# A delta-net kernel's slot order, written anew so that TensorE changes its tile shape four times instead of seven

## The chip, the core and the metric

The kernel runs as one program on one core of a Trainium2 chip. The core has engines that run side by side, each through its own queue in program order: TensorE (PE, matmuls and transposes into PSUM), VectorE (DVE), ScalarE (ACT), GpSimd (POOL) and SyncE (SP, which issues the DMA transfers here). The metric is the time of one execution on the device in microseconds (us). The kernel before takes 4227.17 us, the median of three runs between 4226.82 and 4233.79.

## The reference

The input `x` is 4 sequences of 1024 tokens with 256 channels. It goes through an attention layer of the gated delta-net kind and a feed-forward layer, each between layer norms and with a residual:

```
x = x + layernorm(attn(layernorm(x)))
x = x + layernorm(ffn(layernorm(x)))
```

The attention projects 256 channels to q and k (16 heads of 128 each) and v (32 heads of 128), runs a convolution of four taps over time and a silu, and normalizes q and k. A sequence is cut into 16 chunks of 64 tokens. For each head and chunk, with a lower triangular matrix `A` made of k, beta and a decay, it needs the inverse `Tm` of (1 - A), and then walks through the chunks with a 128 x 128 state:

```
v_new = u_i - kcd_i @ St
out_i = (q_i * exp(g_i)) @ St + attn @ v_new
St    = St * exp(g_last) + (k_i * exp(g_last - g_i)).T @ v_new
```

where `u` is `Tm @ (v * beta)` and `kcd` is `Tm @ (k * beta * exp(g))`. The output is normalized over its 128 channels, multiplied with silu(z), and projected back to 256 channels. The feed-forward layer has 688 inner channels, with weights that are looked up in a table of 16 values. All is float32.

## The kernel before, in words

**Tiling.** Work goes by groups of four v heads (eight groups). A *step* is one chunk of two sequences for one group: 32 steps in a group, 256 in all. The two pairs of sequences alternate, so a step's state was written two steps earlier. Eight steps are a *super block* (32 of them). Two chunks of 64 rows, of two sequences, share the 128 partitions. So many of the matmuls use only a part of TensorE's 128 x 128 array, and several run in it side by side: the profile writes the part as the *tile shape*, rows * columns, such as 64*64.

**Work as generators.** Each piece of work is a Python generator that emits instructions up to its next `yield`. The loop from line 1179 on makes one *slot* per step, and resumes the generators in the order of a string from `SLOTS` (lines 1014 to 1023; eight strings, one for each place in a super block, chosen by `iq`). Each name that goes through `go` counts as a place; a stage that yields a number is resumed by itself so many places later (`resume`, `go`, lines 970 to 990). Under the manual schedule each compute engine gets its instructions in the order in which they are emitted.

**The names in the strings.** A and B are `channel` (line 406): A makes a block of v, B of q or k, many slots ahead. Each has eight matmuls `pp` (128*128), ScalarE's `cv`, and three VectorE instructions of the convolution (line 456) that are resumed later (`far`, then 1). The step (line 780) has the stages N0 (transposes `pv`, and `x0`), N1 (`pkqs`, k and q against the state, then `x0` and `qs`), N2 (`px`, the inverse times x0, then `xs`; here also the transposes of k and ScalarE's `kt`), O3 (`po` and `core`), J (squares of `core`, for the norm), O4 (`pu`, and two places later the new state). N0 to N2 belong to this slot's step, O3, J and O4 to the step before. Z, T and U are `project_out` (line 919) of an older step: `pz` and `zs`, transposes `pto`, and `pout`. Lower-case names: s is `scores` (with `kkq`), n `norms`, v the inverse's rank-one updates on VectorE (`invert`), c `join` and b `build`, which put the inverse together from its blocks in five stages each, with DMAs through memory between them; r and q are the norm's roots on POOL.

**PSUM.** One pool has four banks, which `bank()` hands out in a ring (line 93): each new tile takes the bank of the one four before it, and waits until that has been read. Another has two double banks, for `pp` and `pu` (line 96).

**Loads.** `expand` (line 769) issues the three loads that a step needs, `ue`, `ae` and `qku`, for the next step: at a slot's start, or behind O4 for the first step of a super block.

Of the kernel before, what the change touches and what calls it, by code (L numbers as in the profile page):

```python
# [65 lines left out]
def delta_net_ffn_kernel(  # L66
# [258 lines left out]
    with ExitStack() as main:  # L325
# [80 lines left out]
        def channel(k, blk, n, far):  # L406
# [48 lines left out]
            for i in reversed(range(H)):  # L455
                V.scalar_tensor_tensor(cv, ps[:, :, i : i + BT], cw[:, ch, i : i + 1], cv, ALU.mult, ALU.add)  # L456
                if i == H - 1:
                    yield 1
# [309 lines left out]

        def expand(k, u):

            ue = sc.tile([P, HG, C], F32, tag="ue", name="ue", bufs=NZ)
# [4 lines left out]
            qku = sc.tile([P, 2, 2, MG, C], F32, tag="qku", name="qku", bufs=2)  # L776
            nc.sync.dma_start(qku.rearrange("p j a m t -> p j (a m t)"), k.qkd[:, :, u].rearrange("p j a m t -> p j (a m t)"))
            k.qku[u] = qku

        def step(k, u):  # L780
# [13 lines left out]
            x0 = t4("x0")  # L794
# [4 lines left out]
            if not first:  # L799
# [14 lines left out]
                qs = t4("qs")  # L814
# [5 lines left out]

            ue, ae = k.exp.pop(u)

            pxs = [bank("px") for _ in range(2)]
            if not last:
                for ab in range(2):
                    T_.transpose(pxs[ab][:, 2 * P : 3 * P], qk[:, 0, ab].rearrange("p m t -> p (m t)"), ident)  # L826
# [13 lines left out]
            if not last:  # L840
                kt = sc.tile([P, 2, 2, P], F32, tag="kt", name="kt")
                for ab in range(2):
                    for n in range(2):
                        A.activation(
                            kt[:, ab, n, :],
                            pxs[ab][:, 2 * P : 3 * P],
                            AF.Copy,
                            scale=k.cd[:, ab, blk, un, n : n + 1],
                        )
            yield  # L850
            pos = [bank("po") for _ in range(MG)]
            for n in range(2):
                for m in range(MG):
                    for ab in range(2):
                        T_.matmul(  # L855
                            pos[m][ab * C : (ab + 1) * C, n * P : (n + 1) * P],
                            lhsT=ae[m * C : (m + 1) * C, ab, n, :],
                            rhs=xs[m * C : (m + 1) * C, ab, n, :],
                            start=True,
                            stop=True,  # L860
                        )
            core = t4("core", OUT_LAG)
            for m in range(MG):
                two = slice(2 * m, 2 * m + 2)
                po = pos[m][:, : 2 * P].rearrange("p (h d) -> p h d", h=2)
                if first:
                    V.tensor_copy(core[:, two], po)
                else:
                    V.tensor_tensor(core[:, two], po, qs[:, two], ALU.add)  # L869
            k.cores[u] = core  # L870
            yield
            junk = sc.tile([P, P], F32, tag="junk", name="junk")
            for h in range(HG):
                A.activation(junk, core[:, h, :], AF.Square, accum_out=k.ms[:, u, h : h + 1])  # L874
            yield
            if not last:
# [17 lines left out]
                else:  # L894
                    flat = S_.rearrange("p m a h d -> p (m a h) d")
                    made = pu.rearrange("p a (n d) -> p (a n) d", d=P)
                    for i in range(2 * HG):
                        V.scalar_tensor_tensor(  # L898
                            flat[:, i, :], flat[:, i, :], el[:, ti, i : i + 1], made[:, i, :], ALU.mult, ALU.add
                        )  # L900

# [94 lines left out]
        older, gated, started = None, None, {}  # L996

        def work(kind, n, *args):
# [16 lines left out]
            "c A O3 s N0 n J O4 N1 Z T B n N2 U n s c",  # L1015
            "A O3 N0 J O4 N1 r Z s T B N2 q U c",
            "c A O3 N0 J O4 N1 b Z s T B N2 n U b",
            "A O3 N0 J v1 O4 N1 Z T B N2 U s b",
# [159 lines left out]
        with tc.manual_schedule(engines=COMPUTE):  # L1178
            for s in range(-LQ, len(units)):
# [5 lines left out]
                for c in "01234":  # L1185
                    gens["N" + c], gens["O" + c] = newer, older
# [128 lines left out]
```

## Time and profile before

| | before |
|---|---|
| median of three runs | 4227.17 us |
| the profiled execution, its own time | 4219.99 us |
| its span, first to last instruction | 4218.3 us |
| granted TensorE clock, mean | 0.979 |
| first step's `pv`, last step's `pv` | 252.1 us, 3894.4 us |
| TensorE busy | 3949.9 us |
| VectorE, ScalarE, POOL busy | 2972.5, 2810.3, 1964.5 us |

The profile shows one execution. Busy time is the time in which an engine had an instruction running. Matmuls overlap, and the ends that are shown for them are modelled; what TensorE can do is read better from the starts, one group to the next. A line of the timeline has the start and the length of a group of equal instructions in us, the engine, the line of the kernel, the operation, the tile written and those read, for TensorE its tile shape, and the number of instructions; in brackets, the idle time of the engine before it and what ended that. A line of the list of waits has who waited for whom, the total in us, how often, and the longest.

### The profile page before, as it was taken

To read this page: it belongs to the slowest core of one execution; us is meant where nothing else is said; L and a number is where in the kernel's file an instruction comes from. 1 tells how busy PE (TensorE), PEld (TensorE's weight loads), DVE (VectorE), ACT (ScalarE), POOL (GpSimd) and SP (SyncE) were. 2 spreads that over 40 slices of the span, in tenths; PEclk is the share of its full clock that TensorE was granted. 3 is DMA by queue.
4 is the path that set the end of the run, shared out by engine and by line. 5 is a ranking of instruction groups with operands and counts; after the bars stand their busy time and mean duration, and the time that the engine had idled before them with its cause. 6 is when DMAs were issued, how large, how long until landed. Compare 5 with 4: busy or idle time off the path is not lost.

```text
span 4218.3 us, 96596 instructions
## 1 busy us (share of the span) xinstructions
PE 3949.9 (94%) x34688; PEld 2683.1 (64%) x34688; DVE 2972.5 (70%) x7123; ACT 2810.3 (67%) x7509; POOL 1964.5 (47%) x1808
## 2 busy tenths in 40 slices
PE   3679999999999999999999999999999999999999
PEld 2356666666666666666666666666666666665454
DVE  4577787777777777777777877777777777676143
ACT  2467777777677777777777777777777767665211
POOL 2544555555455545555454555545454334334122
PEclk7889999999999999999999999999999999999999
DMA  3555556565555556665565556655656556553011
GB/s 103 147 126 128 125 134 139 135 143 139 132 145 138 134 133 142 152 138 132 137 148 139 129 139 148 143 134 139 142 141 143 131 132 144 137 130 97 25 46 25
DMA packets 1454779, 539.39 MB, mean 128 GB/s; under 512 B 1119440, under 2 KB 1414496, under 8 KB 1453920
## 3 DMA queue, kind: packets, MB, share of 16 engines
q1 hardware_dynamic: 1454304, 533.20, 53.4%
q8 instruction: 280, 4.59, 0.5%
q14 instruction: 195, 1.60, 0.1%
HBM read 292.82 MB, written 239.62 MB: 126 GB/s over the span
## 4 chain that ended last, share of the span: by engine, by line
PE 73%; DVE 7%; DMA 7%; SPq 4%; ACT 3%; issue 2%; POOL 2%; POOLq 0%; ACTq 0%; DVEq 0%
PE pp L439 17%; PE pout L950 11%; PE pkqs L806 8%; PE pz L145 8%; PE pu L882 5%; PE pgu L1115 4%; PE px L830 3%; PE po L855 3%; DVE cv L456 3%; PE pto L943 3%; DMA ndh<-nbh 3%; PE pv L793 3%; PE py L1131 2%; PE kkq L574 2%; PE px L826 1%
## 5 line engine op out<-in xcount | busy, mean ns | idle before, releaser
L456 DVE SCALAR_TENSOR_TENSOR cv<-pp,cw,cv 128x512 f32<-128x512 f32 x1536 | 1150.7, 749 | 563.4 <-ACT cv L453 527.8
L937 POOL TENSOR_TENSOR zs<-zs,rr 128x512 f32<-128x512 f32 x256 | 267.1, 1043 | 956.4 <-ACT zs L935 956.4
L439 PE MATMUL pp<-xnT,wq 128*128 128x262 f32 x2048 | 509.7, 391 | 49.5 <-DVE cv L456 30.3
L950 PE MATMUL pout<-wo,oT 128*128 128x256 f32 x2048 | 525.4, 401 | 30.0 <-POOL wo L387 14.1
L453 ACT ACTIVATE cv<-pp,cw 128x512 f32<-128x512 f32 x512 | 353.1, 690 | 290.1 <-PE pp L439 285.4
L439 PE MATMUL pp<-xnT,wv 128*128 128x262 f32 x2048 | 519.5, 396 | 26.5 <-DMA wv<-in_wqkv 24.8
L145 PE MATMUL pz<-wzs,xnT 128*64 128x512 f32 x2048 | 484.9, 594 | 6.7 <-DVE core L869 4.6
L898 DVE SCALAR_TENSOR_TENSOR S<-S,dkm,pu 128x128 f32<-128x128 f32 x1792 | 481.0, 342 | 0.0
L806 PE MATMUL pkqs<-S,qku 128*64 128x256 f32 x3840 | 467.7, 385 | 0.7 <-DVE core L869 0.4
L950 PEld LDWEIGHTS pout<-wo,oT 128*128 128x128 f32 x2048 | 378.2, 194 | 123.3 <-ACT cv L453 21.5
L439 PEld LDWEIGHTS pp<-xnT,wv 128*128 128x128 f32 x2048 | 383.8, 193 | 106.4 <-issue 37.7
L439 PEld LDWEIGHTS pp<-xnT,wq 128*128 128x128 f32 x2048 | 373.5, 192 | 111.5 <-issue 45.1
L869 DVE TENSOR_TENSOR core<-po,qs 128x256 f32<-128x256 f32 x480 | 181.2, 418 | 277.1 <-PE po L855 250.2
L874 ACT ACTIVATE junk<-core 128x128 f32<-128x128 f32 x1024 | 315.9, 309 | 54.9 <-DVE core L869 30.2
L806 PEld LDWEIGHTS pkqs<-S,qku 128*64 128x64 f32 x3840 | 254.1, 136 | 134.7 <-issue 1.2
L939 POOL TENSOR_TENSOR zs<-zs,core 128x512 f32<-128x512 f32 x256 | 326.7, 1276 | 20.0
L915 POOL TENSOR_TENSOR rr<-rr,rsqrt 128x16 f32<-128x16 f32 x64 | 187.1, 2923 | 280.3 <-DVE rr L907 280.0
L317 POOL TENSOR_SCALAR lt<-lx,lutb 128x344 f32<-128x344 int32 (+2 forms) x210 | 277.0, 1319 | 16.6
L797 ACT ACTIVATE x<-pv,nnk 128x256 f32<-128x256 f32 x512 | 214.7, 471 | 101.9 <-PE pv L793 100.7
L627 DVE TENSOR_TENSOR v<-v,rank 128x30 f32<-128x30 f32 (+7 forms) x480 | 268.8, 560 | 16.5
L882 PE MATMUL pu<-xs,kt 64*128 64x128 f32 x3840 | 278.9, 285 | 1.0 <-DVE cv L456 1.0
L558 POOL TENSOR_TENSOR dc<-dc,dkm 128x512 f32<-128x512 f32 x128 | 133.8, 1045 | 311.9 <-DMA dc<-rows_d 288.7
(191 smaller groups left out, 6820.5 us busy)
## 6 DMA issues: line engine op xcount, KB each, us to landing
qkd<-qk SPq DMA_DIRECT2D x256, 256.0 KB
qku<-qkd SPq DMA_DIRECT2D x256, 256.0 KB
dc<-rows_d SPq DMA_DIRECT2D x128, 256.0 KB
ltd<-lT SPq DMA_DIRECT2D x128, 256.0 KB
atd<-aT SPq DMA_DIRECT2D x256, 128.0 KB
ae<-atd SPq DMA_DIRECT2D x256, 128.0 KB
ue<-ued SPq DMA_DIRECT2D x256, 128.0 KB
acc_d<-ac SPq DMA_DIRECT2D x128, 256.0 KB
```

Of the source, the lines that this page charges most:

```text
L145: T_.matmul(ps[ab * C : (ab + 1) * C, :], lhsT=xnT[:, kc, 2 * p + ab, H + n * C : H + (n + 1) * C], rhs=rhs(kc), start=kc == 0, stop=kc == ...
L317: G_.tensor_scalar(o[:n, :cols], ix[:n, :cols], float(e), lutb[:n, e : e + 1], ALU.is_equal, ALU.mult)
L439: T_.matmul(ps[:, 2 * p : 2 * p + 2, : H + BT], lhsT=wt[:, kc, :], rhs=xnT[:, kc, 2 * p : 2 * p + 2, c0 : c0 + H + BT], start=kc == 0, sto ...
L453: A.activation(cv, ps[:, :, H : H + BT], AF.Copy, scale=cw[:, ch, H : H + 1])
L456: V.scalar_tensor_tensor(cv, ps[:, :, i : i + BT], cw[:, ch, i : i + 1], cv, ALU.mult, ALU.add)
L627: V.tensor_tensor(to, to, t, ALU.subtract)
L806: T_.matmul(as4(ps)[ab * C : (ab + 1) * C, two, :], lhsT=qk[:, j, ab, m, :], rhs=S_[:, m, ab], start=True, stop=True,)
L874: A.activation(junk, core[:, h, :], AF.Square, accum_out=k.ms[:, u, h : h + 1])
L882: T_.matmul(as4(pu[:, m])[:, 2 * ab + n, :], lhsT=kt[half, ab, n, :], rhs=xs[half, ab, n, :], start=True, stop=True,)
L898: V.scalar_tensor_tensor(flat[:, i, :], flat[:, i, :], el[:, ti, i : i + 1], made[:, i, :], ALU.mult, ALU.add)
L939: G_.tensor_tensor(zs, zs, k.cores.pop(u), ALU.mult)
L950: T_.matmul(pp[:, :HID], lhsT=oT[:, h, :], rhs=wo[:, h, :], start=h == 0, stop=h == HG - 1)
```

## The change

The order within a slot is written anew, and the step is cut into other stages: N0, N1, then X, Y and P for the step before, then O and K for the step before that.

- X is new: it takes the two banks `po`, transposes k into their columns 256 to 383, and makes `kt` from there (four ScalarE instructions). Before, these were part of N2 and used the `px` banks.
- Y is `px` and `xs`. P is `pu` and, two places later, the new state; it now stands before O in the step's order, and at the end of the slot.
- O is `po` and `core`, one slot later than before; it writes columns 0 to 255 of the banks that X of the next step has taken, which are handed over in the list `spare`. K is the squares.
- `x0` and `qs` get two buffers, `qku` three, `ue` two instead of three. `expand` is split: `fetch_qk` loads `qku` for the next step, and `expand` loads `ue` and `ae` for this slot's step, at its start or, for a super block's first step, at its end.
- U belongs to a step one older than T's.
- A's convolution is resumed three places after A instead of two.
- The stages of the inverse (v, c, b), of the scores and of the norms stand in other places, the last ones of `join` and `build` further from one another.

```diff
-        def channel(k, blk, n, far):
+        def channel(k, blk, n, far, near):
...
-                    yield 1
+                    yield near
...
+        def fetch_qk(k, u):
+            qku = sc.tile([P, 2, 2, MG, C], F32, tag="qku", name="qku", bufs=3)
+            nc.sync.dma_start(qku.rearrange("p j a m t -> p j (a m t)"), k.qkd[:, :, u].rearrange("p j a m t -> p j (a m t)"))
+            k.qku[u] = qku
+
         def expand(k, u):
-            ue = sc.tile([P, HG, C], F32, tag="ue", name="ue", bufs=NZ)
+            ue = sc.tile([P, HG, C], F32, tag="ue", name="ue", bufs=2)
...
-            x0 = t4("x0")
+            x0 = t4("x0", 2)
...
-                qs = t4("qs")
+                qs = t4("qs", 2)
...
             yield
 
+            banks = [bank("po") for _ in range(MG)]
+            spare[:] = [banks]
+            if not last:
+                kt = sc.tile([P, 2, 2, P], F32, tag="kt", name="kt")
+                for ab in range(2):
+                    T_.transpose(banks[ab][:, 2 * P : 3 * P], qk[:, 0, ab].rearrange("p m t -> p (m t)"), ident)
+                for ab in range(2):
+                    for n in range(2):
+                        A.activation(
+                            kt[:, ab, n, :],
+                            banks[ab][:, 2 * P : 3 * P],
+                            AF.Copy,
+                            scale=k.cd[:, ab, blk, un, n : n + 1],
+                        )
+            yield
             ue, ae = k.exp.pop(u)
             pxs = [bank("px") for _ in range(2)]
-            if not last:
-                for ab in range(2):
-                    T_.transpose(pxs[ab][:, 2 * P : 3 * P], qk[:, 0, ab].rearrange("p m t -> p (m t)"), ident)
...
+            yield
             if not last:
-                kt = sc.tile([P, 2, 2, P], F32, tag="kt", name="kt")
...
+                pu = two_banks("pu")
...
+                yield 2
+                state = S_.rearrange("p m a h d -> p (m a h d)")
...
             yield
-            pos = [bank("po") for _ in range(MG)]
+            pos = spare.pop() if spare else [bank("po") for _ in range(MG)]
...
         SLOTS = [
-            "c A O3 s N0 n J O4 N1 Z T B n N2 U n s c",
-            "A O3 N0 J O4 N1 r Z s T B N2 q U c",
-            "c A O3 N0 J O4 N1 b Z s T B N2 n U b",
-            "A O3 N0 J v1 O4 N1 Z T B N2 U s b",
-            "A b O3 s N0 n J O4 N1 Z v1 T B n N2 v1 U v1 n s",
-            "A v1 O3 N0 v1 J O4 N1 r Z s v1 T B N2 q v1 U b",
-            "A v1 O3 N0 v1 J O4 N1 Z s v1 T B N2 n v1 U",
-            "A v1 O3 N0 v1 J O4 N1 Z v1 T B N2 v1 c U s",
+            "v1 B N0 n s U c T A n X O Y N1 K Z s P c",
+            "B N0 U T A X O Y N1 K q Z s c P",
+            "B N0 U T A X O Y K N1 r Z s c n P",
+            "B N0 c U T A X O Y N1 K Z b n s P",
+            "v1 b B N0 n s U T A n X O Y N1 K Z s v1 b v1 P",
+            "B N0 v1 U b T v1 A X O Y N1 v1 K Z s v1 b P",
+            "B N0 U v1 T A v1 X O Y K N1 v1 r Z s v1 n P",
+            "B N0 U v1 T A v1 X O Y N1 v1 K Z v1 n s P",
         ]
...
-                    gens["A"] = channel(supers[nv], iv // 4, 2 * MG + iv % 4, 2)
+                    gens["A"] = channel(supers[nv], iv // 4, 2 * MG + iv % 4, 3, 1)
...
-                inv = work(invert, nq - 1)
+                inv = work(invert, nq - 1 if iq >= 4 else nq - 2)
...
-                if ahead and ahead[1]:
-                    expand(*ahead)
+                if 0 <= s + 1 < len(units):
+                    fetch_qk(*units[s + 1])
+                if s >= 0 and i:
+                    expand(*units[s])
...
-                older = newer
+                if s >= 0 and not i:
+                    expand(*units[s])
+                older, oldest = newer, older
...
-            drain(older)
+            for gen in (older, oldest, older, oldest):
+                go(gen)
+            drain(oldest, older)
```

## The prediction

> **What bounds the kernel now.** I read the page first (busy shares), then the idle time of each engine, then the list of waits, then TensorE's timeline of one slot in the middle, and last the starts of its single matmuls there.
>
> ```profile
> PE 3949.9 (94%) x34688; PEld 2683.1 (64%) x34688; DVE 2972.5 (70%) x7123; ACT 2810.3 (67%) x7509; POOL 1964.5 (47%) x1808
> ```
> TensorE is busy 94%; nothing else passes 70%. Between the first step's transposes (252 us) and the last step's (3894 us) TensorE idles little, and the slots repeat to within hundredths of a us. One whole slot, from one `pkqs` to the next, in TensorE's timeline (start, length, engine, line):
>
> ```profile
> 2014.30 1.95 PE L806 MATMUL pkqs<-S,qku 128*64 128x256 f32 x16
> 2016.08 1.89 PE L145 MATMUL pz<-wzs,xnT 128*64 128x512 f32 x8
> 2017.90 0.66 PE L943 MATMUL pto<-ident,zs 128*128 128x128 f32 x4
> 2018.39 1.93 PE L439 MATMUL pp<-xnT,wq 128*128 128x262 f32 x8
> 2020.16 0.38 PE L826 MATMUL px<-ident,qku 128*128 128x128 f32 x2
> 2020.47 0.67 PE L830 MATMUL px<-x,ue 64*64 64x128 f32 x16
> 2021.07 1.99 PE L950 MATMUL pout<-wo,oT 128*128 128x256 f32 x8
> 2022.90 1.93 PE L439 MATMUL pp<-xnT,wv 128*128 128x262 f32 x8
> 2024.76 0.67 PE L855 MATMUL po<-xs,ae 64*64 64x128 f32 x16
> 2025.36 0.66 PE L793 MATMUL pv<-ident,vt 128*128 128x128 f32 x4
> 2025.94 1.16 PE L882 MATMUL pu<-xs,kt 64*128 64x128 f32 x16
> 2027.04 1.95 PE L806 MATMUL pkqs<-S,qku 128*64 128x256 f32 x16
> ```
> Read the starts: each group begins where the one before stops feeding, so a slot is the sum of TensorE's groups, 12.74 us here. The column behind the tile names is the tile shape; it changes seven times. `pp` of `wq` has its own shape on both sides and takes 20.16-18.39 = 1.77; `pp` of `wv`, followed by 64*64, takes 1.86.
>
> The waits that remain are few:
>
> ```profile
> PE px L826 <- ACT zs L935: 39.8, 22, 4.5
> ...
> PE pp L439 <- DMA wv<-in_wqkv: 24.8, 7, 4.0
> ...
> PE px L826 <- DVE aT L585: 10.5, 7, 1.9
> ```
>
> **What a change of shape costs.** From the single starts in that window, against the spacing inside a group. Leaving: `wv` to `po` 311 ns for 221, so 90; a 64*64 group's last round 220 for 109, so 111; `pv` to `pu` 202 for 109, so 93; `pu` to `pkqs` 208 for 112, so 96; `pz` to `pto` 1.818 us for 1.717 where `kkq` (same shape) follows, so 101; `px` transposes to `px` 93. Entering (the first instruction is further from the second): 64*64 51, `pv` 56, `pu` 102, `pkqs` 51, `pto` 57, `pout` 104, and `pp` behind a 128*32 group 104. Old slot: leaving 90+111+93+96+101+93+111 = 695, entering 51+56+102+51+57+51+104 = 472, together 1.167 us. New slot "B N0 U T A X | O Y | N1 Z s | P": `pu` to `pp` 96+104, X to O 93+51, Y to N1 111+51, Z or s to P 101+102, together 0.709. **Saved 0.458 us x 256 steps = 117 us.** The 128*32 groups: `mh1`, `mh2`, `m1` stood inside 128*128 work and now stand between two shapes that change anyway (0.2 saved each), `m2` the other way round (0.2 lost); 2 x 0.2 x 32 super blocks = 13. TensorE alone: **-130 us**.
>
> **What is added on the path.** X of step n-1 transposes into columns 256 to 383 of the two banks that O of step n-2 then writes in columns 0 to 255, and O follows X directly in all eight slots. Between them in program order stand four ScalarE reads of those banks (`kt`). Before, `kt` read the `px` banks after TensorE had written all it would, so the trace shows no read by ScalarE ahead of a TensorE write into other columns of its bank. From below the price is nothing, if only touched columns count. From above, O waits for all four reads. The nearest row is in the gates, where L274 and L276 both only read one bank, ScalarE and VectorE:
>
> ```profile
> 80.13 0.60 ACT L274 ACTIVATE dk<-pgate 128x512 f32<-128x512 f32 x1 [19.23 <-PE pgate L272]
> ...
> 80.76 0.69 DVE L276 COPY dk<-pgate 128x512 f32<-128x512 f32 x1 [2.86 <-ACT dk L274]
> ...
> 86.07 0.69 DVE L276 COPY dk<-pgate 128x512 f32<-128x512 f32 x1 [4.62 <-ACT dk L274]
> ```
> VectorE needs nothing that ScalarE makes there, the matmul had landed at 80.09, VectorE was idle, and yet it starts 33 ns behind ScalarE's end, both times. Two engines hold one bank in turn even for reading, so I take the upper end. These rows touch the same columns; that is what they leave open. The Trainium skill ("PSUM — Partial Sum Buffer", section on bank collisions) says that two engines on one bank and partition quadrant collide also at disjoint columns and that software must keep them apart. By that rule the wait is certain; by rows of the same columns alone the sum could be the first rival's, 4090.
>
> The wait's length, with the rows of an old slot:
>
> ```profile
> 2007.63 0.69 ACT L453 ACTIVATE cv<-pp,cw 128x512 f32<-128x512 f32 x1 [0.64 <-PE pp L439]
> ...
> 2008.45 0.66 ACT L839 ACTIVATE xs<-px 128x256 f32<-128x256 f32 x2
> ...
> 2009.00 1.15 ACT L844 ACTIVATE kt<-px,cd 128x128 f32<-128x128 f32 x4
> ...
> 2012.80 0.76 DVE L869 TENSOR_TENSOR core<-po,qs 128x256 f32<-128x256 f32 x2 [0.16 <-PE po L855]
> ```
> Call the start of X's first transpose 0. A's `pp` ends at 0.16 and `cv` (ScalarE, emitted in A, so ahead of `kt`) runs 0.20 to 0.89. The four `kt` (1.15, overlapping their forerunner by 0.11 as behind `xs`) end at 1.91. TensorE restarted 53 ns after ScalarE's end wherever it waited for it, so O runs from 1.96. Then N1: its first bank is O's first (the ring of four banks goes po, po, px, px, pkqs), so it needs the first `core`. `core` starts 0.77 after `po` starts and its first half takes 0.42: 3.2 at most, 2.9 if O's first half, needing only two of the four `kt`, went ahead. TensorE's own path (O's rest, Y 0.55) gives 2.85. Without the wait N1 would start at 0.31+0.49+0.55 = 1.35. **Stall 1.55 to 1.85, I take 1.7** per slot. In slots 0 and 4 a norm's transposes (4 x 0.109) stand between A and X, so 1.26 there. Behind the waiting `po` on TensorE stand Y, N1, Z, the scores and P; what they feed (`xs`, `x0`, `qs`, `zs`, S) comes later by as much, and no other engine is the bound, so it adds nothing. Steps without `kt` (16 of 256, the end of each group) have none. 180 x 1.7 + 60 x 1.26 = 382: **+382 us**. VectorE's bound on this wait: `core` is emitted ahead of A's conv (due three places after A, behind O), and VectorE's earlier work in the slot (state update 2.15, B's conv 2.32, `ac` 0.41) fits into the 6.6 us from B to X, so it isn't late.
>
> **What the change gives back.** The 39.8 us row comes from `lb`'s copy (L708): ScalarE idled 75.7 us in 32 such copies for the load of `v` from `ndh`, with `zs` queued behind. Between that load and the copy stood A, O3, N0, O4, N1 = 5.8 us; now U, T, A, X, the stall, O, Y, N1, Z = 10.4 us, and 75.7/32 = 2.4 was missing. So that goes. With the waits of `px` and `pout` for `aT`, `oT`, `xs` (10.5+7.8+7.8) and about 1.5 us less in each of seven waits for `wv`, it is 75; I keep 40 to 120 (the other groups' idle may come or stay). Moved DMAs: `qku` is fetched in the same slot as before or earlier, and `ue`, `ae` one slot later for a use one slot later. For a super block's first unit `ue` has 8.7 us instead of about 19; the only wait for it so far is 2.4 us, once, so 0 (32 x 2.4 = 77 if that cover went). SyncE has idle time ahead of each. POOL gets no new work: `rms` and the table pieces (1.3+0.7) move within its slot, at 47%. The squares (1.61) now stand between `qs` and `zs` on ScalarE; `zs` is read by T a slot later, over 5 us of TensorE work behind Z. State update: emitted behind the next slot's B, and N1 that reads it is seven places on, 7 us for 2.15. One more stage in the pipe adds at the end a `po`, `core` and squares, 5 us.
>
> **Sum**, against the profiled execution's 4220.0 (span 4218.3; the median is 7 above): 4220-130+382-75+5 = 4402, and at the median **about 4405 us, 4% slower**.
>
> **Rivals.** (1) *Banks are only kept apart by columns touched*: O runs straight behind X. Left is N1's wait for the first `core`, 1.24 after O's start against 1.04 of O and Y, 0.2 x 256 = 50; 4220-130+50-60+5 = 4085, faster by 3%. For: no row shows different columns. Against: the gates' rows. It decides as soon as the stall per slot stays below some 0.8 us (130+75 over 256). (2) *The wait is there, but shorter, and everything else comes back*: 1.25 per slot (`kt` right behind the transposes, `cv` not ahead) is 180 x 1.25+60 x 0.81 = 274; with 120 back, 4249; within 0.2% only if nearly all 186 us of stalls of the old steps vanish. Against: `cv` is in program order ahead. (3) *VectorE gets in the way as well*: a conv part (0.75) or a rank-one pair of the inverse ahead of `core`, stall 2.1 or more: 180 x 2.1+60 x 1.66 = 478, 50 back, 4525. Against: 70% busy, now with longer slots.
>
> **How the numbers follow.** Forecast 0.80; rival 1 0.12; rival 2 0.04, of which 0.02 within 0.2%; rival 3 0.04. 0.2% (8 us) is about what a measurement of this kernel tells from no change. Faster 0.12, same 0.02, slower 0.86. The range goes from rival 2's 4250 to rival 3's 4520; what it leaves out is rival 1 and the far ends.
>
> **What would show it.** Right: in the new timeline `po` starts some 1.6 us after the `kt` transposes' end, with "ACT kt" as what ended TensorE's idle time, 300 to 450 us of it in the list of waits; slots of about 14 us; four shapes a slot; no `px` behind `zs`. Wrong: `po` 0.2 us behind the transposes while `kt` still runs; then the first rival. If `pkqs` waits for `core` by more than 0.5 us, the third.

## The result, and the profile after

The changed kernel takes 4764.45 us (median of 4 runs, 4754.37 to 4769.12), the kernel before 4226.99 us beside it: a ratio of 1.1264, with a 95% interval of 1.1243 to 1.1286. It is slower, as forecast, but by 537 us where the forecast had 178.

The busy line of the page after, with its span:

```profile
span 4752.7 us, 95765 instructions
...
PE 4109.1 (86%) x34688; PEld 2827.2 (59%) x34688; DVE 2915.6 (61%) x7123; ACT 2779.7 (58%) x7509; POOL 1961.2 (41%) x1808
```

The other engines are busy for as long as before or a little less; their shares fell because the span grew. TensorE is busy for 4109 us where it was 3950, with the same number of instructions and fewer changes of shape. So its instructions look longer, and it also idles more: 644 us instead of 268. Both have to be explained.

TensorE's list of waits, after (engine, what it was about to do, what ended the idle time: us in total, how often, the longest):

```profile
PE po L885 <- ACT kt L832: 289.7, 239, 4.9
PE m L735 <- DMA pad<-vtd: 70.1, 13, 10.3
PE m L735 <- ACT dc L562: 43.6, 10, 5.1
PE m L735 <- DMA pad<-ued: 35.1, 8, 4.9
```

The first row is the wait that the prediction priced. The next three are one wait, that of `m1` in `build`: 31 times, once per super block, 149 us. Before, `m1` waited only once, for 5.0 us. (`dc` is named where it came last by the profile; `m1` reads `mt` and `pad`, not `dc`.) The row `px` behind `zs` of before is down from 39.8 to 0.8 us, as forecast, and `pp` behind the load of `wv` is gone.

One slot of after in TensorE's timeline, an eighth string (start, length, engine, line, tiles, shape; in brackets the idle time before and what ended it):

```profile
2007.25 0.38 PE L829 MATMUL po<-ident,qku 128*128 128x128 f32 x2
2008.72 1.06 PE L885 MATMUL po<-xs,ae 64*64 64x128 f32 x14 [1.08 <-ACT kt L832]
...
2010.33 1.95 PE L809 MATMUL pkqs<-S,qku 128*64 128x256 f32 x16
2012.11 1.89 PE L145 MATMUL pz<-wzs,xnT 128*64 128x512 f32 x8
2013.92 1.16 PE L861 MATMUL pu<-xs,kt 64*128 64x128 f32 x16
2015.01 2.03 PE L439 MATMUL pp<-xnT,wq 128*128 128x262 f32 x8
2016.89 0.60 PE L796 MATMUL pv<-ident,vt 128*128 128x128 f32 x4
```

ScalarE's timeline at the same place:

```profile
2007.48 0.67 ACT L453 ACTIVATE cv<-pp,cw 128x512 f32<-128x512 f32 x1
2008.05 1.13 ACT L832 ACTIVATE kt<-po,cd 128x128 f32<-128x128 f32 x4
```

`po` starts 1.47 us behind X's first transpose, in the middle of the four `kt`: behind the two that read the first bank. Its first matmul waits for the semaphore that the second `kt` updates; its fifth, the first into the other bank, waits again, for the fourth. So it is the program that keeps `po` back, bank by bank; whether the chip would need it, no run shows. From X's first transpose to `pkqs` it is 3.08 us here.

The slots, as medians of the time from one `pv` to the next over 232 steps (the 4th to the 235th, called the middle steps from here on), by the string (us, worked out from the starts in the traces), and their sum:

| string | 1st | 2nd | 3rd | 4th | 5th | 6th | 7th | 8th | 232 steps |
|---|---|---|---|---|---|---|---|---|---|
| before | 15.10 | 14.82 | 15.09 | 14.95 | 14.32 | 14.12 | 13.61 | 12.73 | 3361.3 |
| after | 15.19 | 16.12 | 15.85 | 14.00 | 23.66 | 18.13 | 17.40 | 14.01 | 3836.8 |

The strings also hold other parts of the inverse and of the norms than before, so a comparison by place is rough and only the sum is strict. The first four are within 1.3 us of those of before; the fifth is 9.3 us longer, the sixth and seventh 4 us each. The stall per slot, which the prediction spread evenly, isn't what sets these three apart.

The fifth slot's `m1` in TensorE's timeline:

```profile
2096.16 1.94 PE L735 MATMUL m<-pad,mt 128*32 128x128 f32 x32 [4.19 <-DMA pad<-vtd]
2098.03 1.79 PE L861 MATMUL pu<-xs,kt 64*128 64x128 f32 x16
```

What SyncE issued ahead of it (its DMA queue, after; the second number is the time that the issues take):

```profile
2079.15 0.34 SPq L709 DMA_DIRECT2D vtd<-lb  x1
...
2085.84 5.97 SPq L614 DMA_DIRECT2D lb<-ltd  x4
2091.86 2.29 SPq L726 DMA_DIRECT2D pad<-vtd  x4
2094.19 2.62 SPq L730 DMA_DIRECT2D pad<-ued  x4
```

The same queue of before, a super block's build there:

```profile
2067.09 0.34 SPq L709 DMA_DIRECT2D vtd<-lb  x1
...
2074.98 2.24 SPq L726 DMA_DIRECT2D pad<-vtd  x4
2077.26 2.62 SPq L730 DMA_DIRECT2D pad<-ued  x4
...
2082.58 3.39 SPq L614 DMA_DIRECT2D lb<-ltd  x4
```

Before, the loads of `pad` were issued 7.9 us behind the store of `vtd`, ahead of the inverse's four `lb` loads. After, it is 12.7 us, behind them: the fifth string says "v1 b", and the `v1` issues the `lb` loads, 5.97 us of SyncE's time. `m1` then starts 4.3 us behind the first `pad` issue; before, the median was 8.3 us. TensorE stands still for 4.19 us, and everything in the slot behind it too.

Last, the granted clock. The view of stretches has, for each: its window, its length, the busy time and instructions of PE, PEld, DVE, ACT and POOL, the granted TensorE clock, and the DMA share and rate. After, around that `m1`:

```profile
2092.00:2096.00 4.00, 0.00 (x0) 0.00 (x0) 0.87 (x2) 3.88 (x12) 3.35 (x4) 0.99 0.96 139
2096.00:2099.40 3.40, 3.24 (x44) 2.89 (x46) 2.50 (x3) 1.08 (x2) 3.30 (x4) 0.50 0.77 143
```

Behind the empty 4 us TensorE gets half the clock for 3.4 us (0.50 in the last column but two). So `m1` takes 1.87 us from its start to that of `pu`, and `pu` runs 1.79 us instead of 1.16. That is one source of the longer busy time. The other is `po`, shown with 1.06 us instead of 0.67 because it waits inside for the second half of `kt`.

### The profile page after: what moved, and what is told of

The parts are those of the page before. It is cut to its first block, busy times and chain, and to the rows that moved or that the text cites. A ratio compares the mean times of both kernels' runs of the same rounds, so it can differ in the third digit from the quotient of the medians.

```text
span 4752.7 us, 95765 instructions
## 1 busy us (share of the span) xinstructions
PE 4109.1 (86%) x34688; PEld 2827.2 (59%) x34688; DVE 2915.6 (61%) x7123; ACT 2779.7 (58%) x7509; POOL 1961.2 (41%) x1808
## 4 chain that ended last, share of the span: by engine, by line
PE 53%; ACT 22%; SPq 7%; DVE 7%; POOL 4%; issue 4%; DMA 3%; ACTq 0%; DVEq 0%; POOLq 0%
PE pp L439 11%; PE pkqs L809 9%; PE pout L954 5%; PE pz L145 5%; ACT kt L832 5%; PE pgu L1119 4%; ACT cv L453 3%; PE pu L861 3%; PE po L885 3%; SPq L614 3%; PE px L844 2%; DVE cv L456 2%; ACT junk L904 2%; ACT qs L821 2%; PE kkq L574 2%
## 5 line engine op out<-in xcount | busy, mean ns | idle before, releaser
L439 PE MATMUL pp<-xnT,wq 128*128 128x262 f32 x2048 | 546.7, 410 | 34.8 <-DMA wq<-in_wqkv 19.0
L885 PE MATMUL po<-xs,ae 64*64 64x128 f32 x4096 | 278.8, 294 | 309.2 <-ACT kt L832 289.7
L809 PE MATMUL pkqs<-S,qku 128*64 128x256 f32 x3840 | 520.1, 418 | 6.9 <-DVE core L899 6.2
L439 PE MATMUL pp<-xnT,wv 128*128 128x262 f32 x2048 | 499.5, 385 | 6.4 <-DVE S L877 4.9
L954 PE MATMUL pout<-wo,oT 128*128 128x256 f32 x2048 | 495.8, 385 | 6.8 <-ACT oT L949 5.6
L821 ACT ACTIVATE qs<-pkqs,dkm 128x128 f32<-128x128 f32 x960 | 272.9, 367 | 289.5 <-PE pkqs L809 289.5
L885 PEld LDWEIGHTS po<-xs,ae 64*64 64x64 f32 x4096 | 156.3, 134 | 428.6 <-ACT kt L832 423.2
L809 PEld LDWEIGHTS pkqs<-S,qku 128*64 128x64 f32 x3840 | 276.7, 149 | 194.2 <-DVE core L899 61.8
L853 ACT ACTIVATE xs<-px 128x256 f32<-128x256 f32 x512 | 168.5, 381 | 316.5 <-PE px L844 316.5
L904 ACT ACTIVATE junk<-core 128x128 f32<-128x128 f32 x1024 | 319.8, 312 | 24.2
L861 PEld LDWEIGHTS pu<-xs,kt 64*128 64x128 f32 x3840 | 249.4, 199 | 109.0 <-issue 105.6
```

Source lines behind the costliest of these rows:

```text
L439: T_.matmul(ps[:, 2 * p : 2 * p + 2, : H + BT], lhsT=wt[:, kc, :], rhs=xnT[:, kc, 2 * p : 2 * p + 2, c0 : c0 + H + BT], start=kc == 0, sto ...
L809: T_.matmul(as4(ps)[ab * C : (ab + 1) * C, two, :], lhsT=qk[:, j, ab, m, :], rhs=S_[:, m, ab], start=True, stop=True,)
L821: A.activation(qs[:, h, :], as4(got[1])[:, h, :], AF.Copy, scale=e)
L861: T_.matmul(as4(pu[:, m])[:, 2 * ab + n, :], lhsT=kt[half, ab, n, :], rhs=xs[half, ab, n, :], start=True, stop=True,)
L885: T_.matmul(pos[m][ab * C : (ab + 1) * C, n * P : (n + 1) * P], lhsT=ae[m * C : (m + 1) * C, ab, n, :], rhs=xs[m * C : (m + 1) * C, ab, n, :],
L954: T_.matmul(pp[:, :HID], lhsT=oT[:, h, :], rhs=wo[:, h, :], start=h == 0, stop=h == HG - 1)
```

## The experiments

The theory after this reading: two losses that have nothing to do with each other. `po` waits for `kt` because they share a bank (the prediction's mechanism), and `m1` waits for `pad` because SyncE issues its loads behind the inverse's (new). The rivals: that the first is not the bank but the order of ScalarE's work alone, and that the second is only a consequence of the first.

**`kt` without the bank.** The scaled copies read `qk` in SBUF instead of the transposes in `po`'s banks; the transposes still run, `kt` is k untransposed.

```diff
-                            banks[ab][:, 2 * P : 3 * P],
+                            qk[:, 0, ab].rearrange("p m t -> p (m t)"),
```

> This is the changed kernel with one edit: the four kt instructions of X, same engine, same place, same size, read the q/k tile in SBUF instead of the two po banks. The transposes stay and nobody reads them, so kt and what follows from it has wrong values: the transposed k is left out. Theory (the bank is held by one engine at a time, so po waits for the kt reads of other columns of its banks): the interval from X's first transpose to pkqs falls from the 3.07 us median of the changed kernel to about 1.35 to 1.6 (what is left is the first core), some 400 us of the 445 us above 1.345 that 232 such intervals sum up to go away: 4765 to about 4370. Rival (ScalarE itself or xs is late there, or the ring of banks makes po wait): the interval stays at 3 us and the time within 50 us of 4765. A second rival (po's wait hides other lateness, which comes out behind it): the interval shrinks but pkqs, pz or kkq wait more, and the time falls by less than 200.

4406.29 us against 4222.0, a ratio of 1.0434 (1.0421 to 1.0447). TensorE's timeline of that kernel:

```profile
2025.47 0.38 PE L829 MATMUL po<-ident,qku 128*128 128x128 f32 x2
2025.78 0.67 PE L885 MATMUL po<-xs,ae 64*64 64x128 f32 x16
...
2026.96 1.95 PE L809 MATMUL pkqs<-S,qku 128*64 128x256 f32 x16
```

And ScalarE's:

```profile
2025.67 0.69 ACT L453 ACTIVATE cv<-pp,cw 128x512 f32<-128x512 f32 x1 [0.66 <-PE pp L439]
2026.26 1.26 ACT L832 ACTIVATE kt<-qku,cd 128x128 f32<-128x128 f32 x4
```

`po` starts 0.31 us behind the transposes, before the first `kt`, and `pkqs` 1.49 us behind them. ScalarE's order is the same, its `kt` as late as in after, and nobody waits for it. What held `po` was the read of its bank. The time fell by 358 us where some 400 were expected. TensorE's waits now:

```profile
PE m L735 <- DMA pad<-vtd: 115.7, 20, 10.2
PE pkqs L809 <- DVE core L899: 50.4, 77, 1.3
```

`m1`'s wait is still there, and for `vtd` larger than the 70.1 us of after, so it is no consequence of the first. Without the bank's wait the kernel is still slower than before by 4.3%. The forecast's sum without its 382 us is 4020 (4220-130-75+5), so some 380 us stand here that it had no term for: most of the miss lies beside the bank's wait, not in it.

**`X` further from `O`.** `A` is put between them, so that its eight matmuls cover the reads of `kt`, which are now ahead of `cv` on ScalarE. A's convolution is resumed two places on instead of three, and B's silu one later, so that they keep their places.

```diff
-            yield 2
+            yield 3 if n < 2 * MG else 2
...
-            "B N0 U T A X O Y N1 K q Z s c P",
+            "B N0 U T X A O Y N1 K q Z s c P",
...
-            "B N0 U v1 T A v1 X O Y K N1 v1 r Z s v1 n P",
+            "B N0 U v1 T X A v1 O Y K N1 v1 r Z s v1 n P",
...
-                    gens["A"] = channel(supers[nv], iv // 4, 2 * MG + iv % 4, 3, 1)
+                    gens["A"] = channel(supers[nv], iv // 4, 2 * MG + iv % 4, 2, 1)
```

> The changed kernel with X ahead of A in every string, so that A's 1.77 us of matmuls lie between the transposes and po; A's convolution is resumed two places after A instead of three, so that it stays behind core, and B's silu one place later, so that kt stands ahead of it on ScalarE. Theory (po waits for the kt reads): kt ends 2.25 us after T's start, A at 2.43, so po no longer waits for it; left is pkqs behind the first core, 0.2 us. The time falls by the same 390 to 440 us as where kt reads SBUF, to about 4330 to 4380. Rival (kt is not what po waits for): no fall, or a new wait of the same size.

4457.16 us against 4222.0, 1.0555 (1.0541 to 1.0569) against the 1.1264 of after: 307 us come back, with nothing left out, where 390 to 440 were expected. TensorE's waits:

```profile
PE m L735 <- DMA pad<-vtd: 105.0, 19, 10.2
PE pkqs L809 <- DVE core L899: 76.8, 132, 0.9
...
PE po L885 <- ACT kt L832: 26.9, 28, 2.1
```

The bank's wait fell from 289.7 to 26.9 us. What is new is `core`: `pkqs` waits 76.8 us for it, since instructions of VectorE that the strings put ahead of it come in between. `m1` waits as in the last run.

**The `pad` loads first.** In the fifth string `b` goes ahead of `v1`, and with it the loads of `pad` ahead of the first `lb` loads.

```diff
-            "v1 b B N0 n s U T A n X O Y N1 K Z s v1 b v1 P",
+            "b v1 B N0 n s U T A n X O Y N1 K Z s v1 b v1 P",
```

> The changed kernel with two names swapped in the fifth string of SLOTS: b ahead of v1 at the start of the slot. SyncE then issues build's eight loads of the two pad tiles ahead of the inverse's four loads of lb, which take 6 us of SyncE's time in the changed kernel's trace. Theory (m1's wait of 4.2 to 5.7 us in each super block is this order on SyncE's queue): the waits of m1 for the pads and what came with them (149 us for pad and ACT together in the list of waits, 0.85 us of slow m1 each time) fall below 30 us, and VectorE's wait for lb (112 us in 26) grows by the 5 us that the pads' issue takes, 26 to 31 times; the time falls by 100 to 170 us, to 4600 to 4665. Rival (m1 waits because vtd and ued have only just been stored, whatever is issued between): the wait stays above 3 us each and the time within 40 us of 4765.

4687.18 us against 4222.0, 1.11 (1.1085 to 1.1114). It gives back 1.6 points of the 12.6, 77 us where 100 to 170 were expected. The fifth slot falls from 23.66 to 18.57 us, the waits ahead of `m1` from 131.1 to 28.9 us in the middle steps. But the sixth slot rises from 18.13 to 20.27. Now the `lb` loads are late. VectorE's list of waits, after first, then this kernel:

```profile
DVE rank L625 <- DMA lb<-ltd: 111.9, 26, 7.4
```

```profile
DVE rank L625 <- DMA lb<-ltd: 249.8, 29, 11.1
```

VectorE waits in the inverse's rank-one step for them, and the state update, emitted behind it, comes late for TensorE (`pp` waits 53.3 us for `S`).

**One change of shape less, in the kernel before.** `N0` ahead of `O3` in each of its strings joins `pv` to the 128*128 work of A: six changes instead of seven, and no other work.

```diff
-            "A O3 N0 J O4 N1 r Z s T B N2 q U c",
+            "A N0 O3 J O4 N1 r Z s T B N2 q U c",
```

> The kernel before with N0 ahead of O3 in every string: pv then follows A in the same tile shape and po goes straight to pu, so a slot changes shape six times instead of seven and nothing else moves. Theory (a change of shape costs TensorE a drain and one weight load or matmul that nothing overlaps, as read from the starts): saved are leaving 64*64 for 128*128, 111 ns, less nothing, leaving 128*128 from pv, 93, against leaving it from A, 90, and entering pv, 56: 0.15 us a step, 37 us over 256 steps, 4227 to 4190. Rival (the gaps at a change are only where TensorE happens to wait for another engine, and reappear): within 10 us of 4227.

4208.93 us against 4222.0, 0.9958 (0.9944 to 0.9972). The slots without a wait fall by 0.15 us each: the eighth from 12.73 to 12.58, the seventh from 13.61 to 13.46, the second from 14.82 to 14.67. Over 256 steps that would be 38 us; 13 arrive, so the price of a change rests on these slots and not on the total. In the other slots waits moved: the fourth fell by 1.16, the fifth rose by 0.86, the first by 0.15.

**`build` earlier, alone and with `X` ahead.** In the fourth string `c` goes to the front, and its `b`, which begins the build, from behind Z to behind O. The `b` at the fifth string's start, which issued the `pad` loads ahead of `m1`, goes to the fourth string, behind Z. The first kernel has this alone, the second the edits of `X` ahead too.

```diff
-            "B N0 c U T A X O Y N1 K Z b n s P",
-            "v1 b B N0 n s U T A n X O Y N1 K Z s v1 b v1 P",
+            "c B N0 U T A X O b Y N1 K Z b n s P",
+            "v1 B N0 n s U T A n X O Y N1 K Z s v1 b v1 P",
```

> The changed kernel with build's first two stages earlier, and nothing else: c (the load of v) at the start of the fourth string, b (the copy of v into lb, and its stores) behind O there instead of behind Z, and the next b (the loads of the pads) behind Z instead of at the start of the fifth string, so ahead of the inverse's v1. Theory (the 9.4 us that the fifth slot loses are build's way through memory: copy, store, load, with m1 only a slot behind it, and the norm's squares behind the 2 us copy on ScalarE): the fifth slot falls from 23.7 us to 15 or 16, m1's waits from 149 us to under 20, the wait of po for kt stays at 290 us; 4765 falls by 230 to 290, to about 4475 to 4535. Rival (the time goes to whatever stands behind on SyncE, as where the pads' loads were put ahead of lb's: 77 us off, VectorE late behind lb): the fifth slot gains 5 us or less, the sixth loses 2, 4765 falls by under 120.

> Both repairs: X ahead of A (as in the run with X ahead, 4457) and build's stages earlier as in the run beside this. If the two losses are separate they add: 4457 less 230 to 290, 4170 to 4230, so about the kernel before or up to 1% below it, with TensorE's no-wait slot 0.46 us shorter than before and pkqs waiting 0.2 to 0.3 us for core in most slots. Rival (taking one wait away lets the other grow): over 4280.

Alone: 4629.17 us against 4223.72, 1.0966 (1.0951 to 1.0982). Both: 4329.64 us, 1.0266 (1.0244 to 1.0288). Against the 1.1264 of after that is 3.0 points for the build, 7.1 for X (from the run above), and 10.0 for both together: the two losses add. Neither gave what was expected, 4475 to 4535 and 4170 to 4230. In both kernels the wait ahead of `m1` is gone but for one each (3.8 and 5.0 us), and the fifth slot fell to 16 us as forecast; but the sixth rose, from 18.13 to 21.19 us and, with X ahead, from 16.07 to 19.89 (the table is further down). TensorE's waits with both:

```profile
PE pkqs L809 <- DVE core L899: 81.6, 160, 0.9
PE pto L947 <- POOL zs L943: 57.0, 63, 3.2
PE pp L439 <- DVE S L877: 56.9, 23, 3.5
```

These are the largest; `m1` and `kt` aren't among them, and still it is 2.7% slower than before. The lateness has moved one place down SyncE's queue, to the `lb` loads. VectorE's timeline there, with both:

```profile
1913.65 0.19 DVE L625 TENSOR_TENSOR rank<-v,lb 128x30 f32<-128x30 f32 x1 [7.46 <-POOL zs L941]
...
1916.97 2.14 DVE L877 SCALAR_TENSOR_TENSOR S<-S,dkm,pu 128x128 f32<-128x128 f32 x8
```

VectorE stands 7.46 us in front of the first `rank`, which reads `v` and `lb` (the row names what came last by the profile; VectorE's list of waits has the load of `lb` ahead of `rank` 25 times, 188.1 us in all), and the state update is behind it. TensorE meets that at A's `pp`, which uses the double bank that the update reads:

```profile
1919.17 3.48 PE L439 MATMUL pp<-xnT,wv 128*128 128x262 f32 x8 [3.27 <-DVE S L877]
```

**The rank-one steps later, and `core` first.** On the kernel with both repairs, two `v1` leave the fifth string for the sixth and seventh, so that VectorE meets `lb` later. The second kernel has, beyond that, the norm's `n` (first and fifth string) or a `v1` (the last two) ahead of A instead of between A and O, away from `core`.

```diff
-            "v1 B N0 n s U T X A n O Y N1 K Z s v1 b v1 P",
-            "B N0 v1 U b T X v1 A O Y N1 v1 K Z s v1 b P",
-            "B N0 U v1 T X A v1 O Y K N1 v1 r Z s v1 n P",
+            "v1 B N0 n s U T X A n O Y N1 K Z s b P",
+            "B N0 U b T X v1 A O Y v1 N1 v1 K Z s v1 b v1 P",
+            "B N0 U v1 T X A v1 O Y K N1 v1 r Z s v1 n v1 P",
```

and for the second

```diff
-            "v1 B N0 n s U T X A n O Y N1 K Z s b P",
+            "v1 B N0 n s U T X n A O Y N1 K Z s b P",
...
-            "B N0 U v1 T X A v1 O Y K N1 v1 r Z s v1 n v1 P",
+            "B N0 U v1 T X v1 A O Y K N1 v1 r Z s v1 n v1 P",
```

> The kernel with both repairs (X ahead of A, build earlier; 4330), and two of the inverse's rank-one stages moved out of the fifth string into the sixth and seventh. Theory (its sixth slot loses 5.4 us because VectorE, in program order, stands 7.5 us at the first rank-one product until lb has landed behind the pads on SyncE's queue, and the state update and A's pp behind it): the sixth slot falls from 19.9 us to 14.5 to 15.5, the list of waits loses the 57 us of pp behind S; 4330 falls by 120 to 170, to 4160 to 4210, a little below the kernel before. Rival (the lateness moves one place further): above 4270.

> The same, and what VectorE gets between A and O (a norm's small instructions, a rank-one pair, and with them A's conv one place early) moved ahead of A, so that core is the first thing VectorE meets behind po. Theory (pkqs waits for core, 0.2 us where VectorE is free and 0.9 to 1.0 us in the first, fifth and seventh slot, where it is not): these three slots fall to 0.2 us of wait, 2.2 us a super block, 70 us in all less what the seventh keeps; 4090 to 4150, two to three per cent below the kernel before. Rival (pkqs waits for its bank, not for VectorE's order): no difference to the run beside it.

4338.08 us against 4209.33, 1.0309 (1.0288 to 1.0331), and 4315.56, 1.0252 (1.0234 to 1.0271). The first was meant to gain 120 to 170 us and did not: VectorE's wait for `lb` fell from 188.1 to 3.4 us, and the time stayed. TensorE's first wait of the first, then of the second kernel:

```profile
PE px L844 <- DMA ue<-ued: 83.4, 30, 10.9
```

```profile
PE px L844 <- DMA ue<-ued: 81.3, 30, 10.6
```

The load of `ue` for a super block's first step, issued at the end of the sixth slot behind eight more of the inverse's loads, is now what comes late, once per super block, 2.8 us in the mean. The prediction had named this cover ("32 x 2.4 = 77 if that cover went") and taken it at nothing; in after itself the row is 8.2 us, in the kernels up to here 24.2 at most, and only these two have it in every super block. `core` first did a part of what it should: `pkqs` waits 34.7 us for it where it was 75.4, and the first and fifth slots fell by 0.6 us each; but the sixth rose by 0.45, and of some 70 us expected 22.5 arrived, 0.5%.

**The first step's loads earlier as well.** `expand` for a super block's first step is called behind N1 of the sixth slot instead of at the slot's end, one more `v1` goes from the sixth string to the eighth, and B's silu stands one place later in the sixth slot.

```diff
-            "B N0 U b T X v1 A O Y v1 N1 v1 K Z s v1 b v1 P",
+            "B N0 U b T X v1 A O Y v1 N1 v1 K Z s v1 b P",
...
-            "B N0 U v1 T X v1 A O Y N1 v1 K Z v1 n s P",
+            "B N0 U v1 T X v1 A O Y N1 v1 K Z v1 n s v1 P",
...
-                if s >= 0 and not i:
-                    expand(*units[s])
+                    if name == "N1" and s >= 0 and not i:
+                        expand(*units[s])
```

> The last kernel (4316) with what its trace shows late in the sixth and seventh slot put right: the loads of ue and ae for a super block's first step behind N1 of the sixth slot instead of at its end, so ahead of the inverse's eight xh loads on SyncE (px waited 81 us for ue, 30 times); one rank-one stage from the sixth to the eighth slot, which takes the xh loads out of the sixth; B's silu one place later in the sixth slot, where m2 counts as a place and the silu stood ahead of kt (po waited 1.2 us there). Theory (each of the three is a separate wait): the sixth slot 17.2 to 15, the seventh 17.1 to 14.3, 4.5 to 5 us in each of 31 super blocks, 4316 less 140 to 155: 4160 to 4180, 1% below the kernel before. Rival (SyncE's queue is full there and the lateness moves again): above 4250.

4180.09 us against 4211.0, a ratio of 0.9924 (0.991 to 0.9937): 0.8% below the kernel before, at the upper edge of what was expected, and 12% below the changed one. TensorE's largest waits:

```profile
PE pto L947 <- POOL zs L943: 68.5, 72, 3.2
PE pkqs L809 <- DVE core L899: 42.0, 152, 0.8
```

No load of a super block is waited for any more but two, once each, 6.7 us at most. The three edits were made together, so what each gave isn't shown. The slots of the kernels on the way:

| string | 1st | 2nd | 3rd | 4th | 5th | 6th | 7th | 8th | 232 steps |
|---|---|---|---|---|---|---|---|---|---|
| X ahead | 14.86 | 14.31 | 14.38 | 12.65 | 24.28 | 16.07 | 14.53 | 12.94 | 3557.9 |
| build alone | 15.19 | 16.12 | 15.85 | 14.00 | 16.20 | 21.19 | 16.02 | 14.17 | 3714.7 |
| both | 14.85 | 14.32 | 14.38 | 12.62 | 15.87 | 19.89 | 14.53 | 12.93 | 3425.5 |
| ranks later | 14.85 | 14.32 | 14.38 | 12.60 | 15.87 | 16.74 | 17.26 | 13.57 | 3448.7 |
| core first | 14.23 | 14.32 | 14.38 | 12.59 | 15.24 | 17.19 | 17.15 | 13.20 | 3428.4 |
| first loads too | 14.23 | 14.31 | 14.38 | 12.59 | 15.24 | 16.59 | 14.45 | 13.04 | 3294.4 |

The excess walks from the fifth slot to the sixth and to the seventh, and most of it leaves with the last edit. Up to there each cure of one late load had put another load, or its reader, into its place on the same queue. The last kernel still is some 150 us above the forecast's 4020 without a bank's wait: `pto` waits 68.5 us for `zs`, `pkqs` 42.0 for `core` and 29.2 for `xs`; the rest was not taken apart.

## Why the prediction was right and wrong

**The shape changes: right.** Without their waits the groups of after add up to 12.28 us a slot (`pp` 1.874, `pv` 0.434, `pout` 1.729, `pto` 0.437, `pp` 1.772, X 0.31, `po` 0.487, `px` 0.547, `pkqs` 1.778, `pz` 1.817, `pu` 1.092) against 12.73 before: 0.457 saved, forecast 0.458. Two of these groups never run freely in after: `po` is read in the kernel with `kt` from SBUF, and `px` is its 0.598 of before less the 0.051 of entering, so that one is worked out and not seen. The kernel before with one change less confirms it by itself, 0.15 us for one change; 1.167 us for seven had been 0.167 each.

**`po` waits for `kt`: right in mechanism, the size nearly.** The bank, not the columns, is what the program holds; the kernel with `kt` from SBUF shows that. The Trainium skill ("PSUM — Partial Sum Buffer", section on bank collisions) had said that software must keep two engines apart by bank and quadrant and not by address; this program's waits agree with it as to the bank, no run here has two engines in different quadrants of one bank, and the 1.7 us are the price. X to `pkqs` is 3.065 us in the median where it would be 1.345: 1.72 us, forecast 1.7. In the first and fifth slots it is 2.63, so 1.28, forecast 1.26. The stall's parts differ a little: `po` starts behind two of the four `kt`, not all, and `pkqs` then waits for `core`, which the prediction had as its 2.9 against 3.2. So the list of waits has 289.7 us for `po` behind `kt`, a little under the 300 to 450 that the prediction looked for; the rest stands inside `po` and ahead of `pkqs`. Over the whole run, in the 232 steps that have both X's transposes and `pkqs`, the sum is 445 us, forecast 382 for 240. The surplus is in the second, sixth and seventh slots, 3.6 to 3.7 us from X to `pkqs`. There B's silu stands late on ScalarE, ahead of `cv` and `kt`: in the second and sixth behind a table load of 1.28 us, in the seventh behind a wait for VectorE's convolution (1.85 us in one such slot). The order could be read from the strings and was not counted.

**"What the change gives back. … So that goes": the step that failed.** The waits it named did go: TensorE's idle time in the middle steps that is neither `kt`'s nor `m1`'s fell from 108 to 37 us, so 71, forecast 75 for the whole run. But it followed only one distance of the super block's chain, from the load of `v` to the copy of `lb`, and took the lateness that ended there as gained. The copy feeds a store of `vtd`, that the loads of `pad`, those `m1`. For these stages the sum has no term, so they stood at nothing, although the diff moved them past one another ("SyncE has idle time ahead of each" was said of the moved loads of `qku`, `ue` and `ae`, and of `pad` nothing). In the median, from copy to `pad` issue it became 14.7 us where it was 10.5, since the `lb` loads are issued between: 4.2 us later. And `m1` came nearer: before it stood 18.8 us behind the copy and waited for nothing; after, it would stand 14.7 us behind it without its wait of 4.4 us: 4.1 us earlier. Where `m1` waits it starts 4.4 us behind the `pad` issue; before it was 8.3, so there had been 3.9 us to spare, and the two moves took 8.3. The cost: 131 us of waits ahead of `m1` in the middle steps, and what the clock adds. Putting the `pad` loads first took most of the waits away, putting the build earlier all but one; what stayed late then was the next load on the queue.

**No term for the clock.** Every wait was charged by its length. But after some waits TensorE's clock is halved for 3.4 us: in the middle steps 280 us were granted at half, against 55 before. If a half-speed microsecond does half a microsecond's work, that is up to 113 us more, in the fifth slot (126 us at half), the seventh (61) and the sixth (55) above all.

The account of the middle steps closes nearly: they grew by 475.5 us. The shapes took 118 from that (0.457 x 232 and 12 for the 128*32 groups), and 71 of idle time were given back. The bank put 407 in (the steps among these that have X and `pkqs`), `m1`'s waits 131 (none in these steps before), and the slow clock up to 113, of which up to 18 lie inside the bank's 407. Together that is some 444; about 30 I have not taken apart. The rest of the 534 us of span is outside these steps: the first `pv` comes 8.3 us later, the part behind the last `pv` is 7.8 us longer (forecast 5), and the other steps hold 43.

Two sums of the prediction are loose, without weight for the outcome: with the median 7 us above the profiled execution, 4402 gives 4409 and not 4405; and its second rival comes within 0.2% with 141 to 157 of the 186 us given back, not only with nearly all.

**The rivals.** The first fell: X to `po` without a read of the shared bank is 0.31 us, with it 1.45. The third's mechanism exists but is small: VectorE's work ahead of `core` costs `pkqs` 35 to 82 us in the kernels with X ahead. The second, that all else comes back, was the wrong way round: more was lost, and none of the three had a new wait in `build`. The range ended at 4520 because its far end was a longer stall of the same kind.

## What to carry to other kernels

Where stages of a chain with loads are moved, follow the chain to its end: for each transfer write down where it is issued in its queue, what is issued ahead of it and how long these issues take, and where its first reader stands; a chain whose first distance got longer can have lost more on the second. A queue that issues for many late readers hands lateness on: a cure is found only when the last reader in the queue has its slack, so read the list of waits again after each. And price a wait of TensorE with what follows it: look at the granted clock of the stretch behind it, not only at the idle time.

## What the runs showed of the hardware

A change of tile shape costs TensorE about 0.15 us in this kernel: 0.15 us per slot for one taken out of the kernel before, 0.457, in part worked out, for three changes less. The Trainium skill ("TensorEngine Tiling (Array Packing)", section Key Properties) says that a change of tiling mode drains TensorE; these runs put that number to the change as a whole.

The clock didn't need an idle stretch to fall. In a seventh slot of after, with the wait of `po` for `kt`, TensorE's timeline is

```profile
2125.21 1.06 PE L885 MATMUL po<-xs,ae 64*64 64x128 f32 x14 [1.73 <-ACT kt L832]
...
2126.80 3.55 PE L809 MATMUL pkqs<-S,qku 128*64 128x256 f32 x16
```

and the stretches there, in the columns as above:

```profile
2123.30:2126.70 3.40, 1.59 (x34) 1.04 (x32) 1.90 (x8) 2.23 (x6) 0.00 (x0) 1.00 0.49 123
2126.70:2130.10 3.40, 3.40 (x20) 1.95 (x18) 3.33 (x9) 2.15 (x10) 0.00 (x0) 0.50 0.37 95
```

A stretch of 3.4 us in which TensorE was busy for 1.59 us, 47%, is followed by one at half clock, and in it `pkqs` takes 3.55 us for its 1.95. A wait of 1.73 us thus costs 1.6 us once more. Where the wait was 1.08 us, in the eighth slot shown further up, the stretch had 2.24 us busy, 66%, and the clock stayed:

```profile
2007.21:2010.62 3.41, 2.24 (x39) 1.40 (x39) 1.77 (x8) 2.22 (x7) 0.00 (x0) 1.00 1.03 274
```

In the middle steps of after the clock fell in 29 of 29 fifth slots, in 18 seventh, 16 sixth, 7 second ones, and once each in the third, fourth and eighth. The Trainium skill ("TensorE: Matmul & The Clock Gate", Part 1) has the clock fall after one idle window of some 3.4 us that runs freely; the length agrees, and the case of 1.59 busy us shows that the window need not be empty.

How busy it has to be can be read from the traces of the eleven kernels together. In them the granted clock holds each value for a multiple of 3.41 us, all 1146 times, so each trace can be cut into such stretches. Of those at full clock between 300 and 3800 us, all 216 in which TensorE was busy for less than 41% were followed by one at half clock, 136 of the 314 between 41% and 60.5%, and none of the 10316 above. Between the two bounds the shown busy time doesn't decide; the ends of the matmuls in it are modelled. So a wait costs more than its length where it makes one of these stretches emptier than that, and the same wait can do it or not, as it falls into one stretch or across two.

With the kernel that has all the repairs the middle steps hold 20 us at half clock, less than the 55 of before.
